# Five edits and a new set of scheduling keys in a list-scheduled metaformer kernel

## The chip, the cores and the metric

The kernel runs on one core of a Trainium2 chip, in one launch. The metric is the device time of that core in microseconds; the figure of a kernel is the median over its runs. Beside it stands one profiled execution, whose span (first to last instruction) and device time are given below, because all durations of single instructions come from it.

## The reference

Eight images `x` of 384 channels and 32x32 pixels go through two "metaformer" layers in fp32. Cut to what matters:

```
x = x + mamba(ln_c(x))              # layer 0, token mixer: a selective scan over 1024 tokens
t = t + bitffn(ln_t(t), W1, W2)     # layer 0, channel mixer
x = x + displaced_conv(ln_c(x))     # layer 1, token mixer
t = t + bitffn(ln_t(t), W1, W2)     # layer 1, channel mixer

mamba:  xin, z = split(x @ in_proj); u = silu(conv3(xin)); dt, B, C = u @ x_proj
        dt = softplus(dt @ dt_proj + b)
        h[d,n] = exp(dt[d]*A[d,n]) * h[d,n] + dt[d]*u[d]*B[n]     # 768 channels x 16 states
        y[d]   = sum_n h[d,n]*C[n] + D[d]*u[d];  out = (y * silu(z)) @ out_proj

bitffn: Wb = sign-binarized W, in 5 groups of output rows:
            z = Wg - mean(Wg);  Wb = z + (sign(z) - z)
        y = x @ Wb + b, scaled and clipped by the largest |y| of a batch group; gelu between
```

The clip groups hold one image each (8 // 5 = 1), and images 5 to 7 are left at zero by the quantizer, so that five images need both feed-forward blocks and three need the scan and the displaced convolution alone.

## The kernel before, in words

The scan is cut into 16 units, one for each image and half of its tokens (T = 512). A unit has six channel blocks j of 128 channels, and each of these four steps g, since the 16 states are spread as 4 states x 32 channels over the 128 partitions. That makes 24 steps a unit and 384 in all. One step of `scan` handles four channel groups c, in two pairs p of two:

- GpSimd (POOL) multiplies dt*u by B for each pair (L796, into a tile `t`, 128x1024).
- ScalarE (ACT) makes the four decays exp(dt*A) (L806, into `da` in PSUM, 128x512 each).
- VectorE (DVE) runs four scans of 512 tokens (L821). Those of pair 0 end in `t` in SBUF, those of pair 1 in `da` in PSUM.
- The last column of each scan is kept as the state for the second half of the image. This happens in the eight units that are first halves. ACT copies it for both pairs (L838 for pair 0, L848 for pair 1).
- The product with C: pair 0 by POOL in place in `t` (L842), pair 1 by DVE out of PSUM (L855).
- TensorE (PE) sums over states into `y` (L863), and DVE gates the result (L881, L887).

The tile ring `t` has five buffers, so that POOL can run at most some two steps ahead of PE.

What a unit needs is made by fillers: `in_proj` (L574; its weights come by DMA into the ring `win`, two buffers), a convolution of three taps (L605), `x_proj`, `prep` (softplus, dt*u by POOL at L766), and `spread`, which writes a tile to DRAM (`via`) and reads it back in eight DMAs: two destination tiles (`dts` or `dus`), four 32-partition quarters each. `load_bc` does likewise for B and C, four quarters to a tile `bc`.

The binarization (`binarize`, 4 weight matrices x 5 groups) takes place early in the run, in parallel with the first units: a reduction by DVE, a mean by PE, ACT subtracts it (L1025), DVE takes the sign in two instructions (L1035: z > 0; L1044: (z < 0) minus that, which is minus the sign), and two POOL instructions form z + (sign - z) (L1053, L1060). The feed-forward products L1284 and L1363 read what it writes.

The order of all this isn't in the source as such. Each operation is recorded in a list with an engine, an expected duration, the buffers that it reads and writes, and a key. `Flow.run` then places the operations in a modelled time: each engine takes, among those whose inputs are ready and whose ring buffers are free, the one with the lowest key. The keys are numbers: step k of the scan has keys near k (0 to 384), with offsets `KB`, `KE`, `KC_`, `KY`, `KG` for POOL's product, the decays, the product with C, PE's sum and the gate; the feed-forward blocks and convolutions are spread between the key pairs of `ROWS` and `CONVS`, shifted by engine with `AP`, `AD`, `AA`, `AL`; the binarization between `KI` and `KJ`. `PEN` and `HOLD` make it less ready to change ScalarE's function table; each change is a table load (L301). The result is one fixed instruction order for each engine, with the waits between them. All DMAs stand in one order in SyncE's queue (SP). An operation that writes a part of a tile (`tile[i]`) depends in this list only on what touched that part; one that names the whole tile depends on all earlier ones, also where they write other partitions.

In the chip's program each DMA carries one of eight completion semaphores in turn, and a DMA that takes one again waits for the DMA eight places earlier to land.

Of the kernel before, what the change touches and what calls it, by code (L numbers as in the profile page):

```python
# [11 lines left out]
AF = mybir.ActivationFunctionType  # L12
ALU = mybir.AluOpType
# [4 lines left out]
P = 128  # L18
B, C, HW = 8, 384, 1024
T = 512  # L20
NS = HW // T
KC = C // P
# [4 lines left out]
Q = 4  # L27
D = P // Q
# [8 lines left out]

KB, KE, KC_, KY, KG = -1.26, 0.41, 0.63, -0.65, 0.12  # L40

KP, KR = -6.29, 8.37
KEND, KZ, KL, KX, KXP = -21.77, 35.06, -41.63, -4.58, -8.14

KI, KJ = 203.71, 645.99
EZ, EZ0, EZ1 = 6, -10.51, -9.29

AP, AD, AA, AL = 19.85, -10.33, -3.15, -89.45

PEN = 6.96  # L50

GBS = 260.0


ROWS = [
    [-39.29, 29.81, -200.84, 76.67, 36.06, 113.6, 56.13, 164.05],
    [111.61, 118.31, 160.45, 75.21, 169.64, 118.75, 241.97, 151.58],
    [183.3, 189.97, 259.69, 184.74, 200.63, 260.33, 275.49, 225.23],
    [239.06, 274.78, 286.53, 115.0, 171.23, 298.35, 335.05, 391.82],
    [288.59, 323.09, 393.58, 335.41, 341.02, 380.92, 396.9, 520.17],  # L60
]
CONVS = [
    [317.67, 276.15],
    [565.16, 450.0],
    [591.68, 381.19],
]


# [61 lines left out]
class Flow:  # L130
# [1 line left out]


    SWITCH = 1.5
    HOLD = {"exp": 0.0, "silu": 6.08, "gelu": 0.85, "softplus": 0.0}

    def __init__(self, nc):
        self.nc, self.ops, self.key, self.block = nc, [], 0.0, None
# [166 lines left out]
def metaformer_flow(ctx, tc, x, mw, f0, offset, f1, out):  # L305
# [3 lines left out]
    op, dma = fl.op, fl.dma  # L309
# [4 lines left out]
    def ring(name, shape, bufs, pool=sb, ordered=True, dtype=F32):  # L314
        return Ring([pool.tile(shape, dtype, name=f"{name}{i}") for i in range(bufs)], ordered)

    def one(name, shape, parts=1, pool=sb, dtype=F32):
        return ring(name, shape, 1, pool, dtype=dtype).fixed(parts)
# [25 lines left out]
    y_r = ring("y", [P, T], 1, ps)  # L344


    da = [one("da0", [P, T], 1, ps), one("da1", [P, T], 1, ps), one("da2", [P, 2, T], 1, ps)]
    decay = lambda c: da[c].ap if c < 2 else da[2].ap[:, c - 2, :]
    xn_r = ring("xn", [P, KC, T], 1)
    win_r = ring("win", [P, KC, P], 2)  # L350
    wo_r = ring("wo", [P, JC, P], 1)
# [1 line left out]
    sq_r = ring("sq", [P, KC, T], 1, ordered=False)  # L353
    u_r = ring("u", [P, T], 8)
    xi_r = ring("xi", [P, 2 + T], 2)
    z_r = ring("z", [P, T], 8)
    dbc_r = ring("dbc", [3 * D, T], 2)
    bc_r = ring("bc", [P, 2, T], NG)
    soft_r = ring("soft", [P, T], 3)
# [198 lines left out]
        layernorm(st[i]["xn"], 1e-6)  # L558

    def in_proj(i, m, hold):  # L560
        w = win_r.new()
        dma(
            lambda: w.ap,
            lambda: w_in.rearrange("(k p) o -> p k o", p=P)[:, :, m * P : (m + 1) * P],
            (),
            [w],
            196,
        )
        acc = mm.new()
        xn = st[i]["xn"]  # L570

        def go(e):
            for k in range(KC):
                e.matmul(acc.ap, w.ap[:, k, :], xn.ap[:, k, :], start=(k == 0), stop=(k == KC - 1))  # L574

        op("PE", 2.65, go, [w, xn], [acc], hold=hold)
        return acc
# [126 lines left out]

    def load_bc(i, g):

        t = st[i]["bc", g] = bc_r.new()
        bcd = st[i]["bcd"]

        def src(q):  # L710
            return bcd.ap.rearrange("(r q g) t -> q g r t", r=2, q=Q)[q, g].partition_broadcast(D)

        for q in range(Q):
            dma(lambda q=q: t.ap[q * D : (q + 1) * D], lambda q=q: src(q), [bcd], [t], 128)

    def spread(src, r):

        via = via_r.new()
        dma(lambda: via.ap, lambda: src.ap, [src], [via])
        dst = [r.new(), r.new()]  # L720
        for p in range(2):
            for q in range(Q):
                dma(
                    lambda p=p, q=q: dst[p].ap[q * D : (q + 1) * D],
                    lambda p=p: via.ap.rearrange("(c d) t -> d c t", d=D)[:, 2 * p : 2 * p + 2, :],
                    [via],
                    [dst[p]],
                    128,
                )
        return dst  # L730
# [45 lines left out]
    def scan(i, j, g):  # L776


        b, s = units[i]
        k = i * UNIT + j * NG + g  # L780
        bc = st[i]["bc", g]
        if g == 0:
            y = st[i]["y"] = y_r.new()
        y = st[i]["y"]
        ts = []
        for p in range(2):
            cs = slice(2 * p, 2 * p + 2)
            t = t_r.new()
            ts.append(t)
            dt, du = st[i]["dts", j][p], st[i]["dus", j][p]  # L790
            wide = lambda r: bc.ap[:, r].unsqueeze(1).to_broadcast([P, 2, T])
            fl.key = k + KB + 0.3 * p
            op(
                "POOL",
                2.35,
                lambda e, t=t, du=du: e.tensor_mul(t.ap, du.ap, wide(0)),  # L796
                [du, bc],
                [t],
            )
            for r in range(2):  # L800
                c = 2 * p + r
                fl.key = k + KE + 0.1 * c
                op(
                    "ACT",
                    0.68,
                    lambda e, c=c, r=r, dt=dt: e.activation(  # L806
                        decay(c),
                        dt.ap[:, r, :],
                        AF.Exp,
                        scale=aneg.ap[:, j * Q + c, g : g + 1],  # L810
                    ),
                    [dt, aneg],
                    [da[min(c, 2)]],
                    table="exp",
                )
            for r in range(2):
                c = 2 * p + r
                fl.key = k + 0.1 * c

                def go(e, t=t, c=c, r=r, p=p):  # L820
                    e.tensor_tensor_scan(  # L821
                        t.ap[:, r, :] if p == 0 else decay(c),
                        decay(c),
                        t.ap[:, r, :],
                        0.0 if s == 0 else hst[j][p].ap[:, g, r : r + 1],
                        ALU.mult,
                        ALU.add,
                    )

                first = [] if s == 0 else [hst[j][p][g]]  # L830
                op("DVE", 1.25, go, first + [da[min(c, 2)], t], [t if p == 0 else da[2]])
            fl.key = k + KC_
            if p == 0:
                if s < NS - 1:
                    op(
                        "ACT",
                        0.19,
                        lambda e, t=t: e.copy(hst[j][0].ap[:, g, :], t.ap[:, :, T - 1]),  # L838
                        [t],
                        [hst[j][0][g]],  # L840
                    )
                op("POOL", 2.35, lambda e, t=t: e.tensor_mul(t.ap, t.ap, wide(1)), [bc], [t])  # L842
            else:
                if s < NS - 1:
                    op(
                        "ACT",
                        0.19,
                        lambda e: e.copy(hst[j][1].ap[:, g, :], da[2].ap[:, :, T - 1]),  # L848
                        [da[2]],
                        [hst[j][1][g]],  # L850
                    )
                op(
                    "DVE",
                    1.21,
                    lambda e, t=t: e.tensor_mul(t.ap, da[2].ap, wide(1)),  # L855
                    [bc, da[2]],
                    [t],
                )
        fl.key = k + KY

        def total(e):
            for c in range(Q):
                e.matmul(  # L863
                    y.ap[c * D : (c + 1) * D, :],
                    sel.ap,
                    ts[c // 2].ap[:, c % 2, :],
                    start=(g == 0),
                    stop=(g == NG - 1),
                    tile_position=(0, c * D),
                )  # L870

        op("PE", 1.0, total, [sel] + ts, [y])
# [113 lines left out]
    def binarize(w, dst, kc, o):  # L986
# [6 lines left out]
        for g in range(NQ):  # L993
# [34 lines left out]
                [a],  # L1028
                [z],
            )  # L1030

            op(
                "DVE",
                1.1,
                lambda e, z=z, s=s: e.tensor_scalar(  # L1035
                    s.ap[:, :flat], z.ap[:, :flat], 0.0, None, ALU.is_gt
                ),
                [z],
                [s],
            )  # L1040
            op(
                "DVE",
                1.1,
                lambda e, z=z, s=s: e.scalar_tensor_tensor(  # L1044
                    s.ap[:, :flat], z.ap[:, :flat], 0.0, s.ap[:, :flat], ALU.is_lt, ALU.subtract
                ),
                [z],
                [s],
            )
            op(  # L1050
                "POOL",
                2.1,
                lambda e, z=z, s=s: e.tensor_add(s.ap[:, :flat], s.ap[:, :flat], z.ap[:, :flat]),  # L1053
                [z],
                [s],
            )
            op(
                "POOL",
                2.1,
                lambda e, z=z, s=s: e.tensor_sub(z.ap[:, :flat], z.ap[:, :flat], s.ap[:, :flat]),  # L1060
                [s],
                [z],
            )
# [570 lines left out]
```

## Time and profile before

| what | us |
|---|---|
| median of 3 runs (3773.83 to 3779.07) | 3773.93 |
| profiled execution, device time | 3765.95 |
| its span | 3764.2 |
| POOL busy / DVE busy | 3132.1 / 3171.1 |
| PE busy / ACT busy | 3186.2 / 2568.6 |
| first product of the scan on POOL (L796) begins | 104.4 |
| last product of the scan on POOL (L842) ends | 3656.7 |

Of the 3764 us, the scan thus takes the 3552 in the middle. Counted in the trace, the first L796 of the 16 units (the 1st, 49th, 97th and so on) begin 222.5, 249.5, 242.3, 231.0, 222.9, 210.9, 230.6, 217.6, 213.6, 230.7, 205.4, 208.1, 222.4, 225.3 and 218.4 us after one another, and the last unit takes 198.8. The first three are those in which the binarization and the early projections for the last six units run along.

The page's "idle before, releaser" is the idle time of an engine just before a group of instructions and what ended most of it. A line like "DVE L821" names what finished last; it isn't a proof that nothing else was late.

### The profile page before, as it was taken

Reading aid. Unit: us, or ns where it says so; the run is one execution under the profiler, and the core shown is the slowest. Engines: PE = TensorE matmul, PEld = TensorE weight load, DVE = VectorE, ACT = ScalarE, POOL = GpSimd, SP = SyncE. Lnnn points to the kernel's source line nnn. Section 1 sums busy time; section 2 is a strip of 40 time slices with the busy share of each in tenths; the row PEclk is TensorE's granted clock in tenths of the full one; section 3 lists DMA queues with packets and bytes.
Section 4 is the critical chain, followed back from the end, with each engine's and each line's share of the span. In section 5 each row is a group of like instructions: output and inputs, shape, how many; then the busy total and the mean of one; then the engine's idle time right before and its main releaser. Section 6 shows DMA issues by size and latency. Waiting matters only on the chain.

```text
span 3764.2 us, 35587 instructions
## 1 busy us (share of the span) xinstructions
PE 3186.2 (85%) x9380; PEld 1142.0 (30%) x9380; DVE 3171.1 (84%) x3096; ACT 2568.6 (68%) x3917; POOL 3132.1 (83%) x1488
## 2 busy tenths in 40 slices
PE   5777886987899997799999789997878999867996
PEld 2222222322233332333333233332322333213333
DVE  3788889779897888988887899897899887899984
ACT  4676776766668686776879666777666767766551
POOL 2889889787798888879888887998988898888981
PEclk9787898998899998899999799998979999978997
DMA  8658668685595986768689676878867887968844
GB/s 155 179 147 210 197 175 198 187 238 172 183 253 161 257 235 176 208 189 228 187 236 243 184 210 212 246 206 227 233 203 218 241 239 211 260 172 245 252 139 159
DMA packets 659361, 778.19 MB, mean 207 GB/s; under 512 B 113352, under 2 KB 409176, under 8 KB 659160
## 3 DMA queue, kind: packets, MB, share of 16 engines
q1 hardware_dynamic: 659160, 775.93, 72.9%
q8 instruction: 75, 1.23, 0.1%
q14 instruction: 126, 1.03, 0.1%
HBM read 579.23 MB, written 196.48 MB: 206 GB/s over the span
## 4 chain that ended last, share of the span: by engine, by line
PE 33%; DVE 23%; DMA 14%; ACT 12%; POOL 9%; issue 7%; SPq 2%; POOLq 0%; DVEq 0%; ACTq 0%
PE mm L1284 10%; DVE da L821 8%; PE mm L1363 6%; POOL t L796 6%; PE mm L574 5%; DVE t L821 5%; ACT da L806 4%; PE y L863 4%; PE mm L909 3%; DVE t L855 3%; ACT L301 3%; POOL t L842 2%; DMA bc<-bcd 2%; DMA dts<-via 2%; DMA w<-w2d 2%
## 5 line engine op out<-in xcount | busy, mean ns | idle before, releaser
L796 POOL TENSOR_TENSOR t<-dus,bc 128x1024 f32<-128x1024 f32 x768 | 1808.1, 2375 | 180.7 <-PE y L863 119.5
L806 ACT ACTIVATE da<-dts,aneg 128x512 f32<-128x512 f32 x1536 | 1029.5, 686 | 407.1 <-DVE t L821 201.3
L842 POOL TENSOR_TENSOR t<-t,bc 128x1024 f32<-128x1024 f32 x384 | 909.8, 2370 | 227.0 <-DVE t L821 116.1
L1363 PE MATMUL mm<-hb,w 128*128 128x512 f32 x1440 | 686.7, 616 | 44.2 <-DMA w<-w2d 23.5
L1284 PE MATMUL mm<-tn,w 128*128 128x512 f32 x1440 | 665.0, 608 | 24.8 <-DVE tn L466 11.7
L863 PE MATMUL y<-t,sel 128*32 128x512 f32 x3072 | 540.0, 660 | 136.3 <-DVE t L855 80.1
L821 DVE TENSOR_TENSOR_SCAN da<-da,h,t 128x512 f32<-128x512 f32 x384 | 492.2, 1282 | 89.7 <-ACT da L806 71.7
L301 ACT ACT_TABLE_LOAD x431 | 553.0, 1283 | 7.5
L821 DVE TENSOR_TENSOR_SCAN da<-da,t 128x512 f32<-128x512 f32 x384 | 469.4, 1222 | 72.1 <-ACT da L806 51.3
L821 DVE TENSOR_TENSOR_SCAN t<-da,h,t 128x512 f32<-128x512 f32 x384 | 482.0, 1269 | 53.5 <-POOL t L796 44.8
L821 DVE TENSOR_TENSOR_SCAN t<-da,t 128x512 f32<-128x512 f32 x384 | 458.9, 1208 | 67.3 <-POOL t L796 59.4
L574 PE MATMUL mm<-xn,win 128*128 128x512 f32 x936 | 453.8, 627 | 55.1 <-DMA win<-in_L_conv_in_proj_w 19.6
L855 DVE TENSOR_TENSOR t<-da,bc 128x1024 f32<-128x1024 f32 x384 | 466.1, 1214 | 7.2 <-ACT h L848 2.8
L1363 PEld LDWEIGHTS mm<-hb,w 128*128 128x128 f32 x1440 | 265.7, 194 | 450.7 <-issue 364.6
L1284 PEld LDWEIGHTS mm<-tn,w 128*128 128x128 f32 x1440 | 268.7, 192 | 411.3 <-issue 309.0
L909 PE MATMUL mm<-z,wo 128*128 128x512 f32 x576 | 299.7, 651 | 20.7 <-DVE tr L1433 6.4
L574 PEld LDWEIGHTS mm<-xn,win 128*128 128x128 f32 x936 | 181.5, 200 | 311.3 <-issue 216.8
L1296 ACT ACTIVATE he<-mm,b 128x512 f32<-128x512 f32 x240 | 162.9, 679 | 113.5 <-PE mm L1284 112.6
L863 PEld LDWEIGHTS y<-t,sel 128*32 128x32 f32 x3072 | 80.1, 112 | 499.8 <-issue 176.5
L909 PEld LDWEIGHTS mm<-z,wo 128*128 128x128 f32 x576 | 113.2, 207 | 198.4 <-issue 158.7
L1306 DVE TENSOR_REDUCE sm<-he 128x1 f32<-128x1024 f32 x120 | 144.4, 1203 | 28.6 <-ACT he L1296 28.5
L848 ACT COPY h<-da 128x2 f32<-128x2 f32 x192 | 30.5, 159 | 197.8 <-DVE t L855 101.0
(122 smaller groups left out, 3109.1 us busy)
## 6 DMA issues: line engine op xcount, KB each, us to landing
dts<-via SPq DMA_DIRECT2D x768, 128.0 KB, 4.4
dus<-via SPq DMA_DIRECT2D x768, 128.0 KB, 4.3
hd<-he SPq DMA_DIRECT2D x120, 512.0 KB, 4.2
hb<-hd SPq DMA_DIRECT2D x120, 512.0 KB, 6.0
via<-soft SPq DMA_DIRECT2D x192, 256.0 KB, 3.9
w<-w2d SPq DMA_DIRECT2D x120, 384.0 KB, 4.6
w<-w1d SPq DMA_DIRECT2D x240, 192.0 KB, 3.9
bc<-bcd SPq DMA_DIRECT2D x256, 128.0 KB, 4.8
```

The costliest lines, as they stand in the source:

```text
L301: nc.scalar.preload_act_table_set(SETS[table])
L574: e.matmul(acc.ap, w.ap[:, k, :], xn.ap[:, k, :], start=(k == 0), stop=(k == KC - 1))
L796: lambda e, t=t, du=du: e.tensor_mul(t.ap, du.ap, wide(0)),
L806: lambda e, c=c, r=r, dt=dt: e.activation(decay(c), dt.ap[:, r, :], AF.Exp, scale=aneg.ap[:, j * Q + c, g : g + 1],),
L821: e.tensor_tensor_scan(t.ap[:, r, :] if p == 0 else decay(c), decay(c), t.ap[:, r, :], 0.0 if s == 0 else hst[j][p].ap[:, g, r : r + 1], A ...
L842: op("POOL", 2.35, lambda e, t=t: e.tensor_mul(t.ap, t.ap, wide(1)), [bc], [t])
L855: lambda e, t=t: e.tensor_mul(t.ap, da[2].ap, wide(1)),
L863: e.matmul(y.ap[c * D : (c + 1) * D, :], sel.ap, ts[c // 2].ap[:, c % 2, :], start=(g == 0), stop=(g == NG - 1), tile_position=(0, c * D),)
L909: e.matmul(o.ap, w.ap[:, j, :], zs[j].ap, start=(j == 0), stop=(j == JC - 1))
L1284: e.matmul(acc.ap, w.ap[:, k, :], tn.ap[:, k, :], start=(k == 0), stop=(k == KC - 1),)
L1296: lambda e, he=he, r=r, m=m, acc=acc: e.activation(he.ap[:, r, :], acc.ap, AF.Identity, bias=b1.ap[:, m : m + 1]),
L1363: e.matmul(acc.ap, w.ap[:, part * 2 + r, :], hs[m // 2].ap[:, r * T : (r + 1) * T], start=(m == 0), stop=(m == MC - 1),)
```

## The change

Apart from the keys, and the ring `z` which has seven buffers and no longer eight:

- `load_bc` and `spread` declare each quarter's DMA as a write to one of four parts of the tile and no longer to the whole.
- The sign in the binarization is one ScalarE activation (`AF.Sign`). POOL's two instructions change their signs accordingly (`tensor_sub`, then `tensor_add`).
- The state of pair 0 in the first halves is copied by POOL (`tensor_copy`, 128x2), in front of its product L842. The copy for pair 1, out of PSUM, stays with ACT.
- In the first unit every second `in_proj` takes its weight buffer from the ring `w2` and not from `win`; `w2` isn't used otherwise until the feed-forward blocks start.
- The decays take their PSUM buffers from rings (`da`, two buffers, and `dp`, one of double width) in place of four fixed ones; the memory is the same.
- All the keys have new values, `HOLD` and `PEN` too.

```diff
-KB, KE, KC_, KY, KG = -1.26, 0.41, 0.63, -0.65, 0.12
+KB, KE, KC_, KY, KG = -1.94, 2.22, -0.69, -3.44, -10.11
...
-KI, KJ = 203.71, 645.99
+KI, KJ = 209.23, 394.67
...
-AP, AD, AA, AL = 19.85, -10.33, -3.15, -89.45
-PEN = 6.96
+AP, AD, AA, AL = 38.99, -31.26, -30.79, -121.39
+PEN = 6.76
...
-    HOLD = {"exp": 0.0, "silu": 6.08, "gelu": 0.85, "softplus": 0.0}
+    HOLD = {"exp": 0.0, "silu": 8.58, "gelu": 2.32, "softplus": 0.0}
...
-    da = [one("da0", [P, T], 1, ps), one("da1", [P, T], 1, ps), one("da2", [P, 2, T], 1, ps)]
+    da_r = ring("da", [P, T], 2, ps)
+    dp_r = ring("dp", [P, 2, T], 1, ps)
...
-    z_r = ring("z", [P, T], 8)
+    z_r = ring("z", [P, T], 7)
...
     def in_proj(i, m, hold):
-        w = win_r.new()
+        w = (win_r, w2_r)[i == 0 and m % 2].new()
...
-        t = st[i]["bc", g] = bc_r.new()
+        t = st[i]["bc", g] = bc_r.new(Q)
...
-            dma(lambda q=q: t.ap[q * D : (q + 1) * D], lambda q=q: src(q), [bcd], [t], 128)
+            dma(lambda q=q: t.ap[q * D : (q + 1) * D], lambda q=q: src(q), [bcd], [t[q]], 128)
...
-        dst = [r.new(), r.new()]
+        dst = [r.new(Q), r.new(Q)]
...
-                    [dst[p]],
+                    [dst[p][q]],
...
-                        "ACT",
-                        0.19,
-                        lambda e, t=t: e.copy(hst[j][0].ap[:, g, :], t.ap[:, :, T - 1]),
+                        "POOL",
+                        0.13,
+                        lambda e, t=t: e.tensor_copy(hst[j][0].ap[:, g, :], t.ap[:, :, T - 1]),
...
             op(
-                "DVE",
-                1.1,
-                lambda e, z=z, s=s: e.tensor_scalar(
-                    s.ap[:, :flat], z.ap[:, :flat], 0.0, None, ALU.is_gt
-                ),
-                [z],
-                [s],
-            )
-            op(
-                "DVE",
-                1.1,
-                lambda e, z=z, s=s: e.scalar_tensor_tensor(
-                    s.ap[:, :flat], z.ap[:, :flat], 0.0, s.ap[:, :flat], ALU.is_lt, ALU.subtract
-                ),
+                "ACT",
+                1.0,
+                lambda e, z=z, s=s: e.activation(s.ap[:, :flat], z.ap[:, :flat], AF.Sign),
                 [z],
                 [s],
             )
...
-                lambda e, z=z, s=s: e.tensor_add(s.ap[:, :flat], s.ap[:, :flat], z.ap[:, :flat]),
+                lambda e, z=z, s=s: e.tensor_sub(s.ap[:, :flat], s.ap[:, :flat], z.ap[:, :flat]),
...
-                lambda e, z=z, s=s: e.tensor_sub(z.ap[:, :flat], z.ap[:, :flat], s.ap[:, :flat]),
+                lambda e, z=z, s=s: e.tensor_add(z.ap[:, :flat], z.ap[:, :flat], s.ap[:, :flat]),
```

`ROWS` and `CONVS` (46 numbers) are all new as well; for example the fifth row, for the last image with feed-forward blocks, goes from [288.59, ..., 396.9, 520.17] to [322.68, ..., 542.92, 439.94].

## The prediction

> **What bounds the kernel now.** I read the page's busy shares first, then busy time by stage, then POOL's waits, then the costliest groups, and last the timeline of the places that the edits touch.
>
> ```profile
> PE 3186.2 (85%) x9380; PEld 1142.0 (30%) x9380; DVE 3171.1 (84%) x3096; ACT 2568.6 (68%) x3917; POOL 3132.1 (83%) x1488
> ```
>
> Three engines stand at 83 to 85%, so no share names the bound. The stages, cut at POOL's first and last product of the scan (columns: stretch, its length, busy time and instructions of PE, PEld, DVE, ACT, POOL, then clock, DMA share, GB/s):
>
> ```profile
> 0.00:104.40 104.40, 58.02 (x122) 20.12 (x122) 31.46 (x52) 43.21 (x74) 20.54 (x36) 0.88 0.84 163
> 104.40:660.00 555.60, 426.62 (x1206) 140.69 (x1207) 488.62 (x437) 395.15 (x614) 500.32 (x219) 0.84 0.67 183
> 660.00:3656.70 2996.70, 2631.73 (x7858) 945.69 (x7856) 2601.51 (x2551) 2110.83 (x3201) 2593.66 (x1226) 0.93 0.75 214
> 3656.70:3764.20 107.50, 69.83 (x199) 35.47 (x195) 49.51 (x57) 19.38 (x31) 17.63 (x10) 0.81 0.45 155
> ```
>
> POOL and DVE are 87 to 90% busy all through the scan, and POOL does 72 of the scan's long instructions in each unit. I keep the account on POOL: the span is the start (104.4), POOL's busy time in the scan (500.3 + 2593.7 = 3094.0), its idle time there (3552.3 - 3094.0 = 458.3) and the tail (107.5). What it is idle for (waits by total, times, longest):
>
> ```profile
> POOL t L796 <- PE y L863: 119.5, 69, 10.6
> POOL t L842 <- DVE t L821: 116.1, 51, 7.7
> POOL t L842 <- ACT h L838: 105.4, 44, 7.7
> ...
> POOL t L796 <- DMA dus<-via: 25.3, 6, 9.3
> POOL t L796 <- DMA bc<-bcd: 17.4, 11, 4.3
> ```
>
> Most of it is the scan's own loop: a free `t` (PE after DVE), then DVE's scan. The chain that ended last says the same: PE 33%, DVE 23%, DMA 14%, ACT 12%, POOL 9%; nobody's alone. Then the edited rows:
>
> ```profile
> L1044 DVE SCALAR_TENSOR_TENSOR hb<-hb,hb 128x921 f32<-128x921 f32 (+1 forms) x20 | 38.9, 1947 | 0.2
> L1035 DVE TENSOR_SCALAR hb<-hb 128x921 f32<-128x921 f32 (+1 forms) x20 | 29.6, 1478 | 9.8 <-ACT hb L1025 9.8
> L1025 ACT ACTIVATE hb<-hb,sm 128x921 f32<-128x921 f32 (+1 forms) x20 | 21.1, 1057 | 2.8 <-DVE sm L1016 2.7
> L838 ACT COPY h<-t 128x2 f32<-128x2 f32 x192 | 35.9, 187 | 43.6 <-DVE t L821 40.8 <-POOL t L842 1.1 <-POOL t L796 0.5
> L301 ACT ACT_TABLE_LOAD x431 | 553.0, 1283 | 7.5
> ```
>
> [...] L1035 takes 635 ns at its fastest and 2785 at its slowest, L1044 1078 and 3267; and L796, median 2359 ns, goes to 3295. [...]
>
> **Start.** In the first unit PE waits for weights twice on the way to the scan:
>
> ```profile
> 38.78 8.20 PE L574 MATMUL mm<-xn,win 128*128 128x512 f32 x12 [4.71 <-DMA win<-in_L_conv_in_proj_w]
> 63.10 2.81 PE L574 MATMUL mm<-xn,win 128*128 128x512 f32 x6 [2.66 <-DMA win<-in_L_conv_in_proj_w]
> ...
> 104.37 9.27 POOL L796 TENSOR_TENSOR t<-dus,bc 128x1024 f32<-128x1024 f32 x4 [9.26 <-DMA dus<-via]
> ```
>
> With two more buffers, four weights stand in SP's order ahead of the small loads that hold SP from 11.8 to 31.7; that takes away up to 4.71 + 2.66 = 7.4 us. Then the spreads: now the second `via` is issued at 77.88 and the last quarter of the first `dus` at 99.56, with 32 DMAs in between (0.68 us each), since the list takes the quarters of a tile one after another. In the changed order the same quarter comes 15 DMAs after, the last quarter of `dts` 20 after; 12 fewer at 0.68 are 8 us, of which I take 7, since a 471 KB load stands among them. Start: -14 (bounds -4 and -20).
>
> **Binarization.** DVE loses 40 instructions, 29.6 + 38.9 = 68.5 us. ACT gains 20 of 1.0 us, with a twentieth part of a load; ACT is at 71% there, so this is hidden, and would cost up to 20 us if the decays queued behind it. POOL's two additions stay. [...] mean less median is 2375 - 2359 = 16 ns for 768 L796 and 2370 - 2361 = 9 ns for 384 L842, 12.3 + 3.5 = 15 us. Of POOL's 55.3 us idle in the stage to 660 us, 50 wait for the loop through DVE; with DVE at 488.6 - 60 of 555.6 I take half: -25 (bounds 0 and -50). So DVE's 68.5 aren't the gain; the stage is within 55 us of what POOL itself needs.
>
> **States by POOL.** ACT loses 192 copies (35.9 us). POOL gets them, in front of L842, with L842 and all later products queued behind. No POOL copy is in the trace: the nearest rows are a 128x16 memset (112 ns) and the 128x128 select (295 ns). I take 0.20: 192 x 0.20 = +38 (bounds +20 and +58). The wait on L838 (105.4 in 44 times) is mostly DVE's scan in front of it: ACT's copy starts 0.49 us (median) after the scan ends and takes 0.19, so only 44 x 0.68 = 30 go, and the rest becomes a wait on L821. I take -25. The copy is no pace-setter: units from the fourth on take 218.1 us in the mean (first halves from the fifth: 218.9; second halves from the fourth: 217.5), with copies and without.
>
> **Quarters after the start.** POOL's waits on `dus` and `bc` hold 16.0 + 17.4 us beyond the first unit, on `dts` 5 more. Quarters that stand together in SP's queue still take eight at a time, and the queue's other waits stay. I take -15 (bounds 0 and -38).
>
> **Order.** ACT's list has 395 table loads in place of 432: 37 x 1.283 = 47 us less of ACT. DVE waits 138 us for decays, of which I give the loads and the copies 8 (bounds 0 and -20). How far POOL runs ahead (products L796 issued, less two for each L842) is 3 in 265 of 384 steps, before in 219: slightly steadier, which I count as nothing.
>
> **Tail.** After the last scan PE's list has 36 of the feed-forward's products with L1363's operands, before 2; 28 of them stand ahead of the last product of `end` (L909), on which the last image's convolution hangs. Before, this stretch goes from 3664.4 to 3694.5, 30 us, with PE nearly full. Now 18 of L909 at 0.94 and 28 at 0.96 are 44. Tail: +14 (bounds 0 and +25); six clips of 1.2 leave POOL's scan: -7.
>
> **Sum.** Start 104.4 - 14 = 90.4. Busy 3094.0 - 15 + 38 - 7 = 3110.0. Idle 458.3 - 25 - 25 - 15 - 8 = 385.3. Tail 107.5 + 14 = 121.5. Span 3707.2; the device time lies 1.75 over the span (3765.95 - 3764.2), and the median of the runs 8.0 over the profiled one: 3717.
>
> **Spread.** Units 4 to 16 have the same scan and take 198.8 to 231.0 us, with a standard deviation of 10; a new order draws 16 of them anew, 10 x 4 = 40 us. With half of each pair of bounds above (8, 19, 25, 18, 10, 12) that gives 56, and 1.28 of it 72. The forecast's own range is 3645 to 3755.
>
> **Rivals.** (a) The relief is absorbed: POOL was the pace in the first units, so DVE's freed time turns into waits on POOL, and the idle times stay at 458. [...] -14 - 15 + 38 - 7 + 14 = +16, less the quarters' 15 and the states' 25: 3750. For it speaks POOL's 90% to 660 us; against it that half of its idle time there waits on the loop.
>
> (b) The loop gets looser all over: fewer loads, an ACT without copies and steadier order take another 65 us off POOL's 385: 3652. For it, 235 us of POOL's waits on PE and DVE; against it, the instruction mix after 660 us hardly changes.
>
> (c) Slower: the decays come late. `KE` goes from 0.41 to 2.22, so that ACT's fillers keyed within 1.8 steps now stand ahead of them, and DVE's scan waits on L806 (138 us before, 0.36 a step). At 0.25 us a step more this is 384 x 0.25 = 96: 3813. It decides from 57 / 384 = 0.15 us a step on. For it, the decays have just four PSUM banks and can't be made ahead; against it, runs of five and more other ACT instructions between decays are as rare as before (about 123, before 129).
>
> **Chances.** Forecast 0.5, (a) 0.15, (b) 0.18, (c) 0.17. A difference under 0.2% (7.5 us) can't be told from none here. (a) puts some of its weight near no change: faster 0.77, same 0.06, slower 0.17. The range for 8 in 10 goes from 3640 to 3795.
>
> **What would show it.** First L796 at about 90 us and not 104; no L796 over 2.5 us; the first three units (238 us in the mean) shorter by some 15 us each; a POOL copy of 0.1 to 0.3 us; units with copies no longer than those without; tail about 120 us. Wrong, if later units move from 218 by more than 5, which would be the keys, or if DVE's wait on decays grows past 190 us.

## The result, and the profile after

The changed kernel takes 3737.23 us (median of 4 runs, 3733.09 to 3744.42) against 3773.88 for the kernel before, run beside it. The ratio is 0.9903 with a 95% interval of 0.9883 to 0.9924. It is 1.0% faster, about 37 us. The profiled execution has a device time of 3740.5 and a span of 3738.6.

Most lines of the source moved by one: L797 is the old L796 (POOL's first product), L807 the decays (L806), L822 the scans (L821), L843 POOL's product with C (L842), L856 VectorE's (L855), L864 the sum (L863), L910 the output projection (L909), L1008 the binarization's sum on PE (L1007), L1352 the second feed-forward product (L1363). The state of pair 0 is copied at L839, and L1035 is ScalarE's sign.

The busy line of the page of the changed kernel:

```profile
PE 3177.8 (85%) x9380; PEld 1135.3 (30%) x9380; DVE 3101.4 (83%) x3056; ACT 2520.7 (67%) x3708; POOL 3142.5 (84%) x1680
```

VectorE lost 70 us of work and ScalarE 48, while POOL gained 10 and 192 instructions. Next the stages, cut at the first and last product of the scan on POOL and behind the third unit (columns as before: stretch, length, busy time and instructions of PE, PEld, DVE, ACT, POOL, then clock, DMA share, GB/s). The changed kernel:

```profile
0.00:94.00 94.00, 55.70 (x122) 19.93 (x122) 26.22 (x46) 45.15 (x75) 15.03 (x33) 0.89 0.84 164
...
94.00:756.60 662.60, 541.27 (x1559) 180.87 (x1559) 539.43 (x513) 498.07 (x740) 619.08 (x330) 0.89 0.72 196
756.60:3608.40 2851.80, 2486.82 (x7441) 888.08 (x7442) 2483.47 (x2438) 1947.42 (x2855) 2484.87 (x1305) 0.93 0.75 214
3608.40:3738.60 130.20, 93.99 (x259) 46.42 (x257) 52.25 (x60) 30.07 (x41) 23.56 (x14) 0.90 0.51 170
```

The kernel before, the two stretches of the scan cut at the same place, behind the third unit:

```profile
104.40:818.70 714.30, 572.69 (x1625) 194.52 (x1626) 609.13 (x565) 511.20 (x795) 628.21 (x284) 0.87 0.68 187
818.70:3656.70 2838.00, 2485.66 (x7439) 891.86 (x7437) 2480.99 (x2424) 1994.79 (x3019) 2465.77 (x1161) 0.93 0.75 215
```

The account on POOL that the prediction keeps, read from these lines (busy and idle are those of the scan):

| | start | busy | idle | tail | span |
|---|---|---|---|---|---|
| before | 104.4 | 3094.0 | 458.3 | 107.5 | 3764.2 |
| predicted | 90.4 | 3110.0 | 385.3 | 121.5 | 3707.2 |
| after | 94.0 | 3104.0 | 410.4 | 130.2 | 3738.6 |

The gain sits in the start (10.4) and in the first three units: 714.3 - 662.6 = 51.7 us, with VectorE 70 us less busy there. The other 13 units are 13.8 us longer together, and the tail is 22.7 longer. POOL is 19.1 us busier in these 13 units, since six of them are first halves and now have its copies, and its idle time there is 5.3 us less. -10.4 - 51.7 + 13.8 + 22.7 = -25.6, the difference of the spans.

What POOL waits for in the changed kernel (total, times, longest):

```profile
POOL t L797 <- PE y L864: 128.7, 73, 12.4
POOL t L843 <- DVE t L822: 73.7, 47, 6.9
...
POOL h L839 <- DVE t L822: 69.4, 36, 6.1
...
POOL t L797 <- DMA dts<-via: 32.5, 5, 10.9
```

The wait on ScalarE's copy (105.4) is gone. The wait on VectorE's scan in front of L843 and of the copy before it is now 73.7 + 69.4 = 143.1, against 116.1 + 105.4 = 221.5 on scan and copy before. The wait for a free `t` is no smaller than it was (119.5). Then the edited rows, from the groups by line:

```profile
L797 POOL TENSOR_TENSOR t<-dus,bc 128x1024 f32<-128x1024 f32 x768 | 1796.0, 2358 | 198.8 <-PE y L864 128.7 <-DMA dts<-via 32.5 <-issue 14.7
...
L301 ACT ACT_TABLE_LOAD x393 | 504.2, 1283 | 6.7
...
L839 POOL COPY h<-t 128x2 f32<-128x2 f32 x192 | 36.3, 189 | 69.8 <-DVE t L822 69.4
...
L1035 ACT ACTIVATE hb<-hb 128x921 f32<-128x921 f32 (+1 forms) x20 | 19.3, 964 | 0.3
...
L1035 ACT ACT_TABLE_LOAD x1 | 1.3, 1283 | 0.0
```

The copy takes 0.19 us, the sign 0.96 (1.0 was taken; L1025, over tiles of the same size, took 1.06 before), and no L797 takes longer than 2.41 us, where 17 took over 2.5 before.

Three things are left to ask. What is each edit worth without a change of order? What are the keys worth without the edits? And why do the 13 later units and the tail give back more than half of what the start and the first units win (36.5 of 62.1 us)?

### The profile page after: what moved, and what is told of

Same layout as the page of the kernel before. It is cut to its first block, busy times and chain, and to the rows that moved or that the text cites. A ratio compares the mean times of both kernels' runs of the same rounds, so it can differ in the third digit from the quotient of the medians.

```text
span 3738.6 us, 35437 instructions
## 1 busy us (share of the span) xinstructions
PE 3177.8 (85%) x9380; PEld 1135.3 (30%) x9380; DVE 3101.4 (83%) x3056; ACT 2520.7 (67%) x3708; POOL 3142.5 (84%) x1680
## 5 line engine op out<-in xcount | busy, mean ns | idle before, releaser
L797 POOL TENSOR_TENSOR t<-dus,bc 128x1024 f32<-128x1024 f32 x768 | 1796.0, 2358 | 198.8 <-PE y L864 128.7
L843 POOL TENSOR_TENSOR t<-t,bc 128x1024 f32<-128x1024 f32 x384 | 905.8, 2359 | 83.9 <-DVE t L822 73.7
L1352 PE MATMUL mm<-hb,w 128*128 128x512 f32 x1440 | 681.1, 614 | 32.3 <-DMA w<-w2d 11.2
L864 PE MATMUL y<-t,sel 128*32 128x512 f32 x3072 | 565.8, 657 | 161.8 <-DVE t L856 121.3
L807 ACT ACTIVATE da<-dts,aneg 128x512 f32<-128x512 f32 x768 | 520.9, 684 | 253.5 <-DVE t L822 232.1
L807 ACT ACTIVATE dp<-dts,aneg 128x512 f32<-128x512 f32 x768 | 528.2, 688 | 206.2 <-DVE t L856 193.0
L822 DVE TENSOR_TENSOR_SCAN dp<-dp,h,t 128x512 f32<-128x512 f32 x384 | 491.3, 1279 | 76.3 <-ACT dp L807 66.8
L822 DVE TENSOR_TENSOR_SCAN dp<-dp,t 128x512 f32<-128x512 f32 x384 | 468.8, 1221 | 98.4 <-ACT dp L807 80.2
L822 DVE TENSOR_TENSOR_SCAN t<-da,h,t 128x512 f32<-128x512 f32 x384 | 480.8, 1267 | 58.0 <-POOL t L797 49.3
L822 DVE TENSOR_TENSOR_SCAN t<-da,t 128x512 f32<-128x512 f32 x384 | 459.1, 1207 | 65.3 <-POOL t L797 46.3
L574 PE MATMUL mm<-xn,win 128*128 128x512 f32 x900 | 441.1, 631 | 51.9 <-DVE xn L466 12.1
L856 DVE TENSOR_TENSOR t<-dp,bc 128x1024 f32<-128x1024 f32 x384 | 465.2, 1211 | 6.2 <-ACT h L849 1.9
L1352 PEld LDWEIGHTS mm<-hb,w 128*128 128x128 f32 x1440 | 269.0, 194 | 434.6 <-issue 363.9
L910 PE MATMUL mm<-z,wo 128*128 128x512 f32 x576 | 290.7, 636 | 16.5 <-DMA wo<-in_L_conv_out_proj_w 11.2
L574 PEld LDWEIGHTS mm<-xn,win 128*128 128x128 f32 x900 | 171.2, 199 | 311.1 <-issue 201.4
L864 PEld LDWEIGHTS y<-t,sel 128*32 128x32 f32 x3072 | 86.0, 112 | 545.2 <-DVE t L856 209.8
L413 PE MATMUL mm<-sq,pick 96*128 96x512 f32 x208 | 133.4, 727 | 47.7 <-ACT sq L406 42.9
L910 PEld LDWEIGHTS mm<-z,wo 128*128 128x128 f32 x576 | 108.9, 199 | 186.3 <-issue 154.7
```

The source lines that it names most:

```text
L807: lambda e, c=c, r=r, dt=dt: e.activation(decay(c), dt.ap[:, r, :], AF.Exp, scale=aneg.ap[:, j * Q + c, g : g + 1],),
L822: e.tensor_tensor_scan(t.ap[:, r, :] if p == 0 else decay(c), decay(c), t.ap[:, r, :], 0.0 if s == 0 else hst[j][p].ap[:, g, r : r + 1], A ...
L864: e.matmul(y.ap[c * D : (c + 1) * D, :], sel.ap, ts[c // 2].ap[:, c % 2, :], start=(g == 0), stop=(g == NG - 1), tile_position=(0, c * D),)
L910: e.matmul(o.ap, w.ap[:, j, :], zs[j].ap, start=(j == 0), stop=(j == JC - 1))
L1352: e.matmul(acc.ap, w.ap[:, part * 2 + r, :], hs[m // 2].ap[:, r * T : (r + 1) * T], start=(m == 0), stop=(m == MC - 1),)
```

## Experiments: one edit in a frozen order

A change of an operation's engine or duration moves the whole list. To keep the list, an operation is recorded with its old engine for the planner and only emitted on another one (a new field `on`); all other rows of all engines then stay in place.

**The sign alone, in the order of before.** The planner still sees two VectorE operations; one of them is emitted on ScalarE as the sign, and the other emits nothing. POOL's two signs are turned as in the change.

```diff
-            o.fn(self.on[o.eng])
+            o.fn(self.on[o.on])
...
+            sign = op(
...
-                lambda e, z=z, s=s: e.tensor_scalar(
-                    s.ap[:, :flat], z.ap[:, :flat], 0.0, None, ALU.is_gt
-                ),
...
+                lambda e, z=z, s=s: e.activation(s.ap[:, :flat], z.ap[:, :flat], AF.Sign),
...
+            sign.on = "ACT"
+            op("DVE", 1.1, lambda e: None, [z], [s])
```

> The order of every engine is that of the kernel before; only the sign of the binarization is emitted as one ScalarE activation at the place where the first of the two VectorE instructions stood. Prediction's account: POOL's long products fall back to 2.36 us (none over 2.5), -15 us of POOL's busy time, and up to 25 us of its idle time in the first three units go: 3730 to 3760 against 3774. If the relief is absorbed by POOL as the pace: -15 at most, 3759 to 3770. If the whole gain of the change is in the keys: no change, within 7.

Measured: ratio to before 0.9948, interval 0.9926 to 0.9971, some 20 us. POOL's busy time in the scan falls from 3094.0 to 3078.9, and no L796 is over 2.5 us. Its idle time stays: 458.3 before, 457.2 now. The time lies in the first range of the forecast, but the account is that of its second case. The windows of the first three units, in this kernel:

```profile
103.70:802.90 699.20, 562.60 (x1627) 192.89 (x1628) 551.91 (x532) 526.74 (x813) 612.76 (x283) 0.88 0.69 191
```

Against before, VectorE has 57 us less to do there and the stretch is 15 us shorter, just the 15 by which POOL's busy time fell. Where the rest went is seen in VectorE's waits in this stretch; before:

```profile
DVE da L821 <- ACT da L806: 22.1, 16, 4.6
DVE t L821 <- POOL t L796: 14.6, 9, 4.5
DVE da L821 <- POOL t L796: 10.3, 5, 4.2
```

and with the sign moved:

```profile
DVE da L821 <- ACT da L806: 37.1, 25, 4.6
DVE t L821 <- POOL t L796: 26.7, 18, 4.5
DVE da L821 <- POOL t L796: 16.2, 7, 4.8
```

The freed time became 33 us more of waiting, on the decays and on POOL's product. What is left is POOL's long products: before, all 17 products of L796 and the five of L842 over 2.5 us (2.73 to 3.30, against a median of 2.36) overlap one of VectorE's two instructions in time, and without these the long products are gone. The runs show that the two go together; why isn't shown.

**The same, backwards, in the order of after.** Here the planner sees ScalarE's sign, and VectorE's two instructions are emitted at that place.

```diff
-                "ACT",
-                1.0,
-                lambda e, z=z, s=s: e.activation(s.ap[:, :flat], z.ap[:, :flat], AF.Sign),
...
+            def signs(e, z=z, s=s):
+                e.tensor_scalar(s.ap[:, :flat], z.ap[:, :flat], 0.0, None, ALU.is_gt)
+                e.scalar_tensor_tensor(
+                    s.ap[:, :flat], z.ap[:, :flat], 0.0, s.ap[:, :flat], ALU.is_lt, ALU.subtract
+                )
...
+            op("ACT", 1.0, signs, [z], [s]).on = "DVE"
```

> The changed kernel in its own order, in which only the sign of the binarization goes back to VectorE's two instructions, at the place where ScalarE's stood. Theory [...]: 15 to 24 us slower than the changed kernel, 3752 to 3762; some 16 products of the first kind on POOL over 2.5 us again, POOL's busy time in the scan 12 to 20 us up, its idle time within 10 of 410. Rival (the new order was fitted to a VectorE with 68.5 us less to do in the first units and needs it): 40 us or more slower, 3777 and up, with POOL's idle time of the first units up by 25 or more.

Measured: 3794.43 us; ratio to before 1.0047 (1.0026 to 1.0068), against 0.9903 for the changed kernel. That is 1.0047 / 0.9903 = 1.0145, with the two intervals put together 1.0115 to 1.0175: 55 us are lost. The theory, that as in the order of before the sign is worth only POOL's long products, fell, and the rival holds. The first three units, in this kernel:

```profile
95.00:816.90 721.90, 565.30 (x1555) 188.02 (x1555) 620.00 (x550) 483.74 (x722) 632.78 (x330) 0.87 0.65 180
```

They take 721.9 in place of 662.6. POOL's busy time grows by 13.7 and its idle time by 45.6; over the whole scan it is 13.8 and 38.8. Of POOL's first products 11 take over 2.5 us, where 16 were expected. Every later unit is within 2.4 us of what it was. The waits of PE in this stretch name the path; the changed kernel, then this one:

```profile
PE y L864 <- DVE t L856: 20.1, 9, 8.7
```

```profile
PE y L864 <- DVE t L856: 57.6, 17, 10.9
```

VectorE comes late with its product, so PE's sum comes late, and POOL's wait for a free `t` goes from 17.4 to 35.9 in these units, 18.5 of the 45.6. One thing stays open: PE's granted clock in this stretch is 0.87 where the changed kernel has 0.89, and about as many products (1555 and 1559) keep PE busy for 565.3 in place of 541.3 us. Whether that is a part of the loss or follows from it isn't shown.

So the sign is worth 20 us in one order and 55 in the other. Neither is the whole truth: the first order wasn't made for a VectorE with time to spare, and the second wasn't made for one without. What the sign is worth with keys that suit each case wasn't tried.

**The state's copy alone**, in the order of before, emitted on POOL:

```diff
-                        lambda e, t=t: e.copy(hst[j][0].ap[:, g, :], t.ap[:, :, T - 1]),
+                        lambda e, t=t: e.tensor_copy(hst[j][0].ap[:, g, :], t.ap[:, :, T - 1]),
...
-                    )
+                    ).on = "POOL"
```

> Order of before; the state of pair 0 is copied by GpSimd at the place in the order where ScalarE's copy stood, in front of L842. Prediction's account: +38 of POOL's busy time, -25 of its waits: slower by some 13 us (0 to +33). Rival: the wait on ScalarE is what counts and goes whole: 105 - 38 = faster by up to 65. A third: the copies are hidden in waits on VectorE that are there anyway, no change within 7.

Measured: ratio 0.9997 (0.9986 to 1.0008). POOL is 25.7 us more busy, where 38 were expected, and 21.8 less idle: nothing gained or lost, the third case.

**And backwards, in the order of after**, emitted on ScalarE (the same lines with `copy` and `.on = "ACT"`):

> The changed kernel in its own order, in which only the copy of pair 0's state goes back to ScalarE, emitted at the place in time where GpSimd's stood. Theory (the copy on GpSimd gains as much idle time as it costs busy time, as in the order of before): within 12 us of the changed kernel, 3725 to 3750; POOL's busy time in the scan down by 30 to 40, its idle time up by about as much. Rival 1 (the changed order lives on the copy being off ScalarE, whose decays then come late): 30 us or more slower, with VectorE's waits on decays up from 170 to over 200. Rival 2 (the 36 us are lost on POOL): 3700 to 3715, faster than both kernels.

Measured: 3750.46 us; ratio to before 0.9919 (0.9894 to 0.9945). Over the changed kernel's that is 1.0016, and with its interval (0.9983 to 1.0049) it can't be told from none. The medians lie 13 us apart, half a microsecond beyond what the theory allowed. POOL's busy time falls by 27.5, where 30 to 40 were expected, and its idle time grows by 41.4; VectorE's waits on decays are 147.4 + 23.2 = 170.6, as in the changed kernel (147.0 + 22.9). Both rivals are out: the copy isn't what the decays wait for, and its cost on POOL isn't lost.

## Experiments: edits without keys, keys without edits

Here the list is made anew each time. **The changed code with the old keys** (`KB` to `KXP`, `KI` to `EZ1`, `AP` to `AL`, `PEN`, `HOLD`, `ROWS` and `CONVS` as before), in short:

```diff
-KB, KE, KC_, KY, KG = -1.94, 2.22, -0.69, -3.44, -10.11
+KB, KE, KC_, KY, KG = -1.26, 0.41, 0.63, -0.65, 0.12
...
-KI, KJ = 209.23, 394.67
+KI, KJ = 203.71, 645.99
```

> All edits with the keys, HOLD and PEN of before. Prediction's account counts the keys as nothing but the tail's +14 and the table loads' -8: so 3717 - 14 + 8 = 3711 by its own sizes, or by the measured total some 3731. If the keys make the gain: 3774 or above. In either case a new order lies some 40 us around.

**The old code with the new keys** (the same lines the other way round):

> The kernel before with the new keys, HOLD and PEN and none of the edits. If the edits make the gain: 3774 or a little slower (tail +14, table loads -8: 3780). If the keys make it: near 3737.

Two of the edits alone, with the old keys: **the quarters**,

```diff
-        t = st[i]["bc", g] = bc_r.new()
+        t = st[i]["bc", g] = bc_r.new(Q)
...
-        dst = [r.new(), r.new()]
+        dst = [r.new(Q), r.new(Q)]
```

(and the two DMA calls as in the change),

> The kernel before with quarters noted as parts, old keys. The edit acts through the list's order alone. Prediction's size: start -7, later waits on dts, dus and bc -15: about 3752, if order counts for nothing. If the order decides: anywhere from 3720 to 3880, with the later waits on these DMAs hardly different, and the difference in other waits.

and **the second ring of weights**:

```diff
-        w = win_r.new()
+        w = (win_r, w2_r)[i == 0 and m % 2].new()
```

(and the load fills only the first blocks of the buffer, `w.ap[:, :KC, :]`).

> The kernel before with the first unit's weights on two rings, old keys. The first L796 begins some 7 us earlier than 104.4 (weights come in time), the rest by order: 3725 to 3815. If the start is set by the spreads alone: 104 as before.

| kernel | ratio to before (interval) | start | busy | idle | tail |
|---|---|---|---|---|---|
| edits, old keys | 1.0270 (1.0248 to 1.0293) | 96.8 | 3109.1 | 536.0 | 131.4 |
| new keys, old code | 1.0135 (1.0116 to 1.0155) | 103.7 | 3087.4 | 493.0 | 141.1 |
| quarters, old keys | 1.0238 (1.0195 to 1.0281) | 97.8 | 3091.9 | 549.7 | 116.6 |
| second ring, old keys | 1.0441 (1.0401 to 1.0482) | 102.1 | 3103.6 | 636.7 | 106.7 |

All four are slower than before, by 51 to 166 us. Three lose it mainly as POOL's idle time in the scan, 78 to 178 us more; the old code with the new keys loses 35 there and 34 in the tail. At the start the quarters do what was predicted of them, 6.6 us for 7, and the ring alone only 2.3 for 7. The list that results is worse all the same. The wait for a free `t` shows it, first with the changed code and old keys, then with the ring alone:

```profile
POOL t L797 <- PE y L864: 198.5, 78, 22.2
```

```profile
POOL t L796 <- PE y L863: 279.1, 97, 29.9
```

Against 119.5 us before and a longest of 10.6, POOL now stands up to 30 us at a time in front of a sum that stands behind other work on PE: in the longest, with the ring alone, PE does first feed-forward products for most of the time:

```profile
704.18 23.34 PE L1284 MATMUL mm<-tn,w 128*128 128x512 f32 x54
```

**Is it the edits that do this, or any new order?** Two keys of the kernel before moved a little, no edit at all (the forecast speaks of three and names these two):

```diff
-KEND, KZ, KL, KX, KXP = -21.77, 35.06, -41.63, -4.58, -8.14
+KEND, KZ, KL, KX, KXP = -21.77, 34.06, -41.63, -5.08, -8.14
```

> The kernel before with three keys' offsets nudged (KZ 35.06 to 34.06, KX -4.58 to -5.08) and no edit: some 30% of the instructions change places. If a new order is worth the 40 us that the prediction took from the spread of the units: 3734 to 3814, either way. If old keys and old code are fitted to each other: slower by 20 to 100. If order counts for little: within 10.

and four others:

```diff
-AP, AD, AA, AL = 19.85, -10.33, -3.15, -89.45
+AP, AD, AA, AL = 20.35, -10.83, -3.65, -88.95
```

> The kernel before with four other keys moved a little (the engine offsets: AP 19.85 to 20.35, AD -10.33 to -10.83, AA -3.15 to -3.65, AL -89.45 to -88.95), no edit. Theory (keys fitted to one list): 20 to 120 us slower than before, 3794 to 3894, as POOL's idle time in the scan. Rival (the first jitter's 107 us was one bad draw; a moved order costs as often as it gains, about 40 us either way): within 40 us of before, and as likely faster.

and the changed kernel, with the same step as the first:

```diff
-KEND, KZ, KL, KX, KXP = 1.37, 29.78, -17.46, -1.44, -3.76
+KEND, KZ, KL, KX, KXP = 1.37, 28.78, -17.46, -1.94, -3.76
```

> The changed kernel with two of its keys moved a little (KZ 29.78 to 28.78, KX -1.44 to -1.94), no other edit. Theory (the keys are fitted to one exact list, so that any other order loses, as the same step did with the kernel before, which lost 107 us): 50 to 150 us slower than the changed kernel, 3790 to 3890, the loss being POOL's idle time in the scan. Rival (the quarters, rings and moved instructions make the list robust, so that order matters less now): within 40 us, under 3777.

Measured: the first 1.0285 (1.0247 to 1.0323), the second 1.0124 (1.0096 to 1.0153), the third 1.0288 (1.0257 to 1.0318) over before, which is 1.039 over the changed kernel. So steps of one or a half in keys that run to 384 cost 108, 47 and some 145 us. In the first two POOL's idle time in the scan carries it (563.5 and 504.5 against 458.3), with 10 us of the tail in one and 13 in the other. The third was expected to lose there alone and didn't: idle 488.4, 78 more than in the changed kernel, and a tail of 209.0, 79 more, since more feed-forward work is left for after the scan: PE has 418 products there, 200 of them the feed-forward's, where the changed kernel has 259 and 84. In this one try the new code is no more tolerant of order than the old.

## Experiment: the tail

The last output projection is done in six operations of two products for each column block, and the feed-forward products stand between them. The experiment makes one operation of the six products of a block and half:

```diff
-            for a in range(0, JC, 2):
+            n = JC if i == len(units) - 1 else 2
+            for a in range(0, JC, n):
...
-                    for j in (a, a + 1):
+                    for j in range(a, a + n):
```

> The changed kernel; in the last unit alone the six products of one column block of the output projection are one operation of the list, so that the feed-forward's products can't stand between them. All orders before the last gate are those of the changed kernel. If the interleaving holds up the last image's convolution, as the prediction says: the tail (130.2 after the last product L843) shrinks by 10 to 20 us, 3717 to 3730 against 3737. If the tail is set by the feed-forward's own end (its clip waits 47.8 us): no change or slower.

Measured: 3747.98 us; ratio to before 0.9922 (0.9893 to 0.9952), no gain over the changed kernel. PE in the tail of the kernel before (start, duration), the last sum and the projection after it:

```profile
3664.37 1.06 PE L863 MATMUL y<-t,sel 128*32 128x512 f32 x8
3665.37 1.98 PE L1363 MATMUL mm<-hb,w 128*128 128x512 f32 x4
3667.19 1.88 PE L909 MATMUL mm<-z,wo 128*128 128x512 f32 x4
...
3690.94 3.60 PE L909 MATMUL mm<-z,wo 128*128 128x512 f32 x8
```

and of the changed kernel:

```profile
3613.38 1.07 PE L864 MATMUL y<-t,sel 128*32 128x512 f32 x8
3614.37 3.70 PE L1352 MATMUL mm<-hb,w 128*128 128x512 f32 x8
3617.91 1.88 PE L910 MATMUL mm<-z,wo 128*128 128x512 f32 x4
...
3653.58 1.88 PE L910 MATMUL mm<-z,wo 128*128 128x512 f32 x4
3655.30 4.88 PE L1352 MATMUL mm<-hb,w 128*128 128x512 f32 x11
```

From the last sum to the last product of the projection it is 29.1 us before and 41.1 after. In the experiment it is 29.4; but the feed-forward products, and their weight loads in SP's queue, then stand ahead of the last image's convolution: the rest of the tail is 98 us in place of 83. So the interleaving isn't what holds the tail, and the second case of the text above came true.

Over the kernels here the tail goes with the number of the feed-forward's products that PE has in it: 20 and 107.5 us (before), 52 and 116.6 (the quarters), 57 and 120.8 (the second step of keys), 73 and 131.4 (edits, old keys), 84 and 130.2 (changed), 102 and 141.1 (new keys), 200 and 209.0 (the third step). Two kernels have none in it and tails of 106.7 and 117.7, so something else moves it too; the amount was not varied by itself.

## Why the prediction came out as it did

The direction and the range were right (3717 predicted, range 3640 to 3795, 3737 measured); the gain was 37 us where 57 were predicted. The predicted span was 31.4 us short: start 3.6, busy -6.0, idle 25.1, tail 8.7. The allowance of 8.0 from one execution to the median then took 11 back, by luck, since the profiled execution of the changed kernel lies 3.3 above its median.

**The term that failed** is that of the order. The prediction counted it "as nothing" and gave it only a spread of 40 us. One estimate of its size: over the whole scan, in the order of after, the sign is worth 38.8 us of POOL's idle time and the copy 41.4, 80 together, and the whole idle time fell by 47.9; so the rest of the list, the quarters, the ring and the loads among it, gave 32 back, where the prediction counted 23 of gain for quarters and loads. (It takes the two effects as additive, which was not tried.) By unit, POOL's idle time falls by 42.6 in the first three and grows by 25 in the fifth and 17 in the last. In the first three PE has 66 products fewer than before, in the fifth and the last 80 and 49 more: the new list moves the other work about.

And ±40, from the scatter of the units, was too small a spread for a list made anew: six such kernels took 47 to 166 us more than before, all to one side, and a seventh 145 more than the changed kernel. That the new list came out well is what one would see of keys fitted to these edits, since neither half does it alone and the small steps tried from either list lose; how the keys were found isn't shown here. Nothing in the prediction's working could tell that the new keys were good ones, so that it came near is in part luck.

**Start**: 10.4 of 14. The split was off. The store of the second `via` is issued at 76.81, 1.1 us earlier than before, not 7.4. PE's waits for weights are gone, but PE now waits 6.1 us in front of the binarization's sum L1008, with the next projection behind it in its queue. The profile names ScalarE (L1130); VectorE's reduction for this sum ends at 43.69, just before. PE in the changed kernel:

```profile
43.84 0.56 PE L1008 MATMUL mm<-sm,ones 128*128 128x1 f32 x2 [6.09 <-ACT hb L1130]
```

So POOL's product, whose result that store carries, begins only 2.6 us earlier, before and after:

```profile
75.64 1.26 POOL L766 TENSOR_TENSOR soft<-soft,u 128x512 f32<-128x512 f32 x1 [6.82 <-ACT soft L753]
```

```profile
73.02 1.27 POOL L766 TENSOR_TENSOR soft<-soft,u 128x512 f32<-128x512 f32 x1 [12.84 <-ACT soft L753]
```

Another 1.5 us go in SP's queue, where the store is issued 2.5 us after that product ends, and 1.0 before. SP's queue before, then in the changed kernel:

```profile
76.78 0.37 SPq L193 DMA_DIRECT2D via<-soft  x1
77.25 0.39 SPq L193 DMA_DIRECT2D win<-in_L_conv_in_proj_w  x1
77.88 1.04 SPq L193 DMA_DIRECT2D via<-soft  x2
```

```profile
67.59 6.84 SPq L193 DMA_DIRECT2D bc<-bcd  x14
74.84 0.34 SPq L193 DMA_DIRECT2D via<-soft  x1
75.32 1.16 SPq L193 DMA_DIRECT2D bc<-bcd  x2
76.81 0.82 SPq L193 DMA_DIRECT2D via<-soft  x2
```

From the store to the first product it is 17.2 us against 26.5: that stretch gave 9.3, where 7 were counted for the quarters.

**Binarization**: the 15 us that the prediction took off POOL's busy time, from the mean and the median of its products, were right to a tenth (15.1 in the frozen order). The 25 of idle time stand between two measured ends, about 1 in the old order and 39 in the new. The first three units are 17 shorter each, 15 were predicted. ScalarE's 20 signs are not free: VectorE's waits on decays rise from 139 to 170 us over the whole run, and 29 of that stand in the first three units, which have most of the signs (27.1 before, 56.3 after). Of these waits the sign alone adds 15 in the old order (27.1 to 42.5), and putting it back takes off 8 in the new (56.3 to 48.1). The total stays under the 190 named.

**States**: the copy takes 0.19 us (0.20 taken). POOL's busy time shows only 27.5 us of it in place of 38, since a part of the copies overlaps a neighbour on POOL (8.4 us more overlap than with the copies on ScalarE). But 106 of the products behind a copy begin some 80 ns after it, and about 9 us of such gaps count as idle time; with them the price is near 37. The idle time that it takes away was 21.8 and 41.4 for 25 predicted. The finding, nothing gained or little, is near what the prediction's 38 against 25 said. That first halves should not be longer than second ones was wrong: from the fifth unit on they take 226.3 against 212.8 us. It isn't the copies, since with them back on ScalarE it is 226.6 against 214.3. The largest part is the fifth unit (253.5 in place of 222.9), the one with 80 more products on PE. The prediction's reading of before mixed two counts: its 217.5 for second halves begins at the fourth unit; from the fifth on it was 218.9 against 215.6.

**Tail**: 22.7 for 14. The stretch with the projection grew by 12.0, near what was worked out (44 predicted, 41.1 measured), the time ahead of it fell by 2.7, and the other 13.4 lie behind the projection, before the end, and were not counted. The mechanism did not hold: with the stretch cut back to 29.4 the tail is no shorter.

Of the rivals, (a) is what the sign does in the old order, where the relief is absorbed in waits of VectorE on POOL and the decays; in the new order POOL's idle time does fall. (Its sum says that the idle times stay at 458, and then takes 40 us off them.) (b) doesn't show: in the 13 later units POOL's idle time falls by 5 us. Nor does (c), late decays from `KE`: in these units VectorE's waits on decays are 113.7 against 112.2. (The decays' four buffers did hold up ScalarE: before, it waited in front of L806 for VectorE's L821 201.3 us and for its L855 178.2.) Later units moved from 218.3 to 219.4 in the mean, within the 5 named; but a mean that stands still hid single units that moved by -26 to +31.

No kernel here ran below the changed one.

## What to carry to other kernels

In a list like this one an edit can't be priced alone: here its local gain was in places right to the microsecond, and the new list still lost several times as much with keys not made for it. Measure an edit in a frozen order, both ways, to see how far its worth depends on the order, and move a key without any edit to learn how much a mere change of order costs. Time freed on an engine counts only where the order lets its follower use it; look for it in that engine's own waits.

## What the runs showed of the hardware

A GpSimd copy of 128x2 takes 175 to 217 ns (median 186). In 81 of 192 cases the next POOL instruction starts up to 77 ns before it ends: at 103.16 us a copy of 0.21 us starts, and the next product at 103.30. In 106 cases the next is the product in place in the tile that the copy reads, and it starts 79 to 85 ns after the copy's end. In POOL's busy time over the scan a copy costs 27.5 / 192 = 0.14 us, and with these gaps about 0.19. With VectorE's signs put back, all else in place, four copies take 585 to 630 ns, and all four overlap one of VectorE's sign instructions, as the long products do.

Taking VectorE's 40 sign instructions away shortens no undisturbed product (the median of POOL's first product is 2358 ns without them in the order of before, and 2359 with them); it takes away the 17 long ones. Before, 27 of these products overlap a sign instruction: the 17 (2737 to 3295 ns) and 10 that take 2333 to 2367; of the 741 others none takes over 2439. L1035 and L1044 take 635 to 643 and 1120 ns in the three pairs with no POOL instruction beside them, and up to 2785 and 3267 in the others. The scans (L821) show nothing of this: they stay within 1183 to 1305.

In the traces of both kernels the 3413 DMAs carry eight completion semaphores in turn, and each of the 2979 for which the trace has the landing of the DMA eight places earlier is issued after that landing.
